# Moving one ScalarE operation, the sum of s_i and mask, behind four softmax divisions in a graph-attention kernel

## The chip, the cores and the metric

The kernel runs on one core of a Trainium2 chip. A core has a matrix engine (TensorE, PE in the profile; its weight loads are listed apart as PEld), three engines for elementwise work (VectorE or DVE, ScalarE or ACT, GpSimd or POOL), and a queue, SyncE or SP, from which nearly all transfers here are issued. Each engine goes through its own list of instructions, and semaphores tie the lists together. The metric is the device time of one execution in microseconds. Before the change it is 2422.0 us, the median of three runs (2419.04, 2422.00, 2422.31).

## What is computed

There are 128 graphs of 128 nodes with 512 features, and two layers. Layer 0 is multi-head attention with 8 heads, masked by the adjacency matrix. Layer 1 is a single-head graph attention. Each is followed by a residual addition and a layer normalization without weights. Cut to what matters:

```
# layer 0
q, k, v = x @ Wq + bq, x @ Wk + bk, x @ Wv + bv          # 8 heads of 64
logits  = where(adj > 0, q k^T / 8, -1e9)
attn    = softmax(logits, axis=-1)
x       = layernorm(x + relu((attn v) @ Wo + bo))

# layer 1
Wh  = x @ W
e   = leaky(s_i[:, None] + s_j[None, :])     # s_i = Wh @ a1, s_j = Wh @ a2, leaky slope 0.2
e   = where(adj > 0, e, -9e15)
att = softmax(e, axis=1)                     # over the senders i
x   = layernorm(x + leaky(att @ Wh))
```

## The kernel before, in words

Everything is done in float32. The work on a graph ("block" b) is cut into stages, and one loop over `t` runs different stages of different graphs side by side: the softmax of layer 0 for block t, its attention for block t - 1, layer 0's output product for a pair of blocks starting at t - 3 (odd t), the product with W for the pair at t - 6 (even t), and the edge softmax of layer 1 for blocks near t - 6. The projections q, k, v are made for four blocks at a time, and their pieces are spread over four steps. The loop runs to t = 123; the last four blocks follow a written list of pieces (`PLAN`). The order of instructions on every engine is the order of the program text (`manual_schedule`); no scheduler moves anything.

All large products use Strassen's scheme: seven products p1 to p7 of half-size blocks instead of eight, accumulated in PSUM banks with the roles y, w and x. The same bank y serves p1, p6, p7 and p4 in turn, so ScalarE has to copy it out (`t0`, `t2`, `t3`) before TensorE may write it again:

- `group_product` (matmuls at line 364, copies at 341 and 345, `st_` tiles) makes q, k, v. The weights of v don't fit on chip; their seven blocks come through a ring of three tiles `wv_n` (line 405).
- `pair_product` (matmuls at line 445, copies `pr_t` at line 456) makes the output product of layer 0 in odd steps and x @ W in even ones. Its pieces are taken one by one with `pair()`. The copy `t3` is made in the `pair()` between divisions 5 and 6; the product p4 overwrites the bank it reads.

In x @ W (class `LayerOne`), W has one column more, so that s_i and s_j come out as the last columns of the two halves of `wh`. For the even block of a pair the half with s_i is added by VectorE (line 766) in the same step in which it is used; for the odd block ScalarE copies it (line 764) late in the even step, for use in the following odd one.

The softmax of layer 0 (class `Softmax`, tile `pa`, 128 queries x 8 heads x 128 keys): VectorE adds the mask to the scores (line 530) and takes the maxima (539); ScalarE takes the exponential of each head and its sum (`exp`, line 550, eight instructions); VectorE takes the reciprocals of the sums for heads 0 to 3 and 4 to 7 (`reciprocals`, line 560); ScalarE multiplies each head by its reciprocal (`divide`, line 564, eight instructions). `pa` is then stored to memory (571), read back in blocks (577), and transposed by VectorE (581).

The edge softmax (class `Edge`): `sender` (line 792) is a ScalarE activation that adds s_i, a column of `wh`, to the mask and makes the tile `e`. `store_sender` (800) stores it, `fetch_sender` (806) reads it back in blocks as `ez`, and `turn_blocks` (811) transposes it on VectorE at the start of the next step. Then `add` (814) adds s_j, and the maxima (819, 821), exponential (825), and division (829, 830) follow.

Within a step the SP queue issues the output store (859), the store of `e` (800), often a weight block (405), the store of `pa` (571), the four reads of `ez` (806) and the four reads of `pa` (577), in this order.

Of the kernel before, what the change touches and what calls it, by code (L numbers as in the profile page):

```python
# [24 lines left out]
def kernel(  # L25
# [114 lines left out]
    def load_blocks(*args, **kwargs):  # L140
        for load in block_loads(*args, **kwargs):
            load()
# [4 lines left out]
    def right_blocks(t):  # L147

        return [
            lambda: nc.vector.tensor_sub(t[2], t[2], t[0]),  # L150
            lambda: nc.vector.tensor_sub(t[5], t[3], t[2]),
            lambda: nc.vector.tensor_sub(t[4], t[5], t[0]),
            lambda: nc.vector.tensor_sub(t[6], t[1], t[5]),
        ]

    def places(w):
        return [w[:, n] for n in range(7)]

    def columns(w):
        return w[:, 0:2], w[:, 2:4]  # L160
# [23 lines left out]
    def load_bias():  # L184
        nc.sync.dma_start(bo_b, bo.partition_broadcast(P))
        return [lambda: nc.vector.tensor_sub(bo_b[:, HALF:], bo_b[:, HALF:], bo_b[:, :HALF])]
# [61 lines left out]
    def load_x(b):  # L248
        X[b] = spread(x[b])

    def load_residual(b):

        X1[b] = work.tile([P, D], F32, name="x1", bufs=7)
        nc.sync.dma_start(X1[b], x[b])

    def transpose_x(b):
        g, j = divmod(b, GROUP)
        if j == 0:
            XT[g] = big.tile([P, NC, GROUP * P], F32, name="xT")
        transpose_blocks(XT[g][:, :, j * P : (j + 1) * P], X.pop(b))  # L260

    def sum_x(g):
        sums = big.tile([P, 3, 2, 2 * P], F32, name="xS")
        XS[g], ops = left_blocks(XT[g], sums)
        return lambda: [op() for op in ops]
# [219 lines left out]
    def load_mask(b):  # L485
        MF[b] = small.tile([P, P], I32, name="adj", bufs=2)
        nc.sync.dma_start(MF[b], adj[b])

    def mask_float(b):
        a = MF[b]  # L490
        MF[b] = small.tile([P, P], BF16, name="mf", bufs=9)
        nc.scalar.copy(MF[b], a)

    def mask(b):
        nc.vector.tensor_scalar(MF[b], MF[b], 0.0, BIG, ALU.is_le, ALU.mult)
# [366 lines left out]
    def on(b):  # L862
        return 0 <= b < B
# [19 lines left out]
    def turn_x1(t):  # L883
        layer = zero.pop((t - 4) // 2)
        layer.transpose(0)
        layer.transpose(1)
        sums.append(layer)

    def x1_sums():
        while sums:  # L890
            sums.pop().sum(0, 1, 2, 3)
# [3 lines left out]
    sm = fin = edge = coming = none  # L895

    def x_turns(t):
        if t < 0:
            return {-3: (), -2: (4,), -1: (5, 6, 7)}[t]
        return [b for b in [(), (t + 7, t + 8), (t + 8,), (t + 8,)][t % GROUP] if on(b)]  # L900
# [64 lines left out]
    for t in range(-3, END):  # L965
        pair_steps = []
        if t % GROUP == 1 and on(t + 3):
            rest = group_steps
            group_steps, v_pieces, fetch_v = products((t + 3) // GROUP)
            group_steps = rest + group_steps  # L970
        if t % 2 == 1 and on(t - 3):
            pair_steps = zero[(t - 3) // 2] = LayerZero((t - 3) // 2)
            pair_steps = pair_steps.steps()
        if t % 2 == 0 and on(t - 6):
            pair_steps = LayerOne((t - 6) // 2).steps()

        def group(n=1):
            for _ in range(min(n, len(group_steps))):
                group_steps.pop(0)()
            for _ in range(min((3 if t == -3 else 2 if t >= 1 else 1) * n, len(chores))):  # L980
                chores.pop(0)()

        def w1_chores(n):
            for op in [w1_sums.pop(0) for _ in range(n)]:
                op()

        def pair(n=1):
            for _ in range(min(n, len(pair_steps))):
                pair_steps.pop(0)()

        if on(t + 1):
            load_mask(t + 1)
        if t == 0:
            load_blocks(Wo, columns(wo), nc.sync, spread_rows=False)
            late_chores = right_blocks(places(wo)) + load_bias()
        if t == 1:
            w1_loads, w1_sums = load_w1()
            for chore in late_chores:
                chores += [w1_loads.pop(0), chore]
            chores += w1_loads  # L1000

        last, sm = sm, Softmax(t, first_homes if t in (0, 2, 4) else None) if on(t) else none
        sm.scores()
        coming.turn_blocks()
        if t % 2 == 1 and on(t - 3):
            zero[(t - 3) // 2].by()
            zero[(t - 3) // 2].bw()
        if later and t > 4:
            later.pop().go_back()
        if t == 5:  # L1010
            group(2)
        if t < 3:
            sm.maxima()
            group(2)
            if on(t - 2):
                load_residual(t - 2)
            if t == 0 and on(GROUP):
                sum_x(1)()
            sm.exp(0, 1, 2, 3)
            last.transpose()  # L1020
            group()
            sm.reciprocals(0)
            sm.exp(4, 5, 6, 7)
            if t == 1:
                group()
            sm.reciprocals(1)
            sm.divide(0, 1, 2, 3)
            group()
            sm.divide(4, 5, 6, 7)
            if t == 1:  # L1030
                group()
            if on(t + 1):
                mask_float(t + 1)
        elif t == 4:

            layer = later.pop()
            sm.maxima()
            group()
            layer.apply(0)
            load_residual(2)  # L1040
            if on(8):
                sum_x(2)()
            sm.exp(0, 1)
            group()
            sm.exp(2, 3, 4, 5)
            last.transpose()
            group()
            layer.store(1)
            layer.store(0)
            layer.fetch(1)  # L1050
            layer.fetch(0)
            sm.exp(6, 7)
            group()
            sm.reciprocals(0)
            sm.reciprocals(1)
            sm.divide(0, 1, 2, 3, 4, 5, 6, 7)
            mask_float(5)
        else:
            sm.maxima()
            group()  # L1060
            if t == 5:
                turn_x1(4)
                x1_sums()
            edge = coming
            edge.add()
            fin.residual()
            if on(t - 2):
                load_residual(t - 2)
            edge.maxima()
            fin.stats()  # L1070
            fin.rstd()
            x1_sums()
            if t % GROUP == 0 and on(t + GROUP):
                sum_x(t // GROUP + 1)()
            pair()
            sm.exp(0, 1, 2, 3)
            edge.exp()
            pair()
            sm.exp(4, 5)
            last.transpose()  # L1080
            group()
            sm.reciprocals(0)
            pair()
            sm.exp(6)
            fin.apply()
            fin.store()
            sm.exp(7)
            edge.divide()
            pair()
            sm.reciprocals(1)  # L1090
            coming = Edge(t - 6) if on(t - 6) and t + 1 < END else none
            coming.sender()
            coming.store_sender()
            sm.divide(0, 1, 2, 3)
            if t == 3:
                w1_chores(4)
            group()
            sm.divide(4, 5)
            pair()
            sm.divide(6, 7)  # L1100
            if on(t + 1):
                mask_float(t + 1)
            group()
            if t in (3, 5):
                w1_chores(4 if t == 3 else 8)
        sm.store()
        if t >= 6:
            coming.fetch_sender()
        sm.fetch()
        for b in x_turns(t):  # L1110
            transpose_x(b)
        for b in x_turns(t + 1):
            load_x(b)
        if on(t + 1):
            mask(t + 1)
        pair(2)
        if t % 2 == 0 and on(t - 6):
            turn_x1(t)
        if t not in (0, 4):
            group(21 if t % GROUP == 0 else 1)  # L1120
        fin = edge
        fin.product()
        fin.copy()

        last.attend()
        last.copy()
        if t % 2 == 0:
            last.sum(0, 1, 2, 3)
# [183 lines left out]
```

## Time and profile before

| engine | busy us | share of the span |
|---|---|---|
| TensorE, matmuls | 2368.3 | 98% |
| TensorE, weight loads | 1975.1 | 82% |
| VectorE | 1827.5 | 76% |
| ScalarE | 1515.2 | 63% |
| GpSimd | 812.7 | 34% |

The profiled span is 2418.1 us at a mean granted TensorE clock of 0.998. Some groups of instructions that the text uses:

| operation, line | times | one, us |
|---|---|---|
| sender `e` on ScalarE, 792 | 117 | 0.398 (median) |
| division `pa` on ScalarE, 564 | 1008 | 0.392 (mean) |
| exponential `pa` on ScalarE, 550 | 1008 | 0.394 (mean), and 0.191 for reading the sum |
| copy `pr_t` on ScalarE, 456 | 375 | 0.366 (mean) |
| store of `e`, 64 KB, 800 | 117 | 1.8 to landing (median) |
| reading `ez`, 4 x 16 KB, 806 | 468 | 2.2 to landing (median) |
| weight block `wv_n`, 256 KB, 405 | 224 | 2.8 to landing (median) |

A "wait" in the profile is idle time of an engine just before an instruction, put down to what released it last. A line of the timeline gives the start in us, the duration in us, the engine, the line of the kernel, the operation, the tiles (out<-in), the shapes, how often it was repeated, and in brackets the idle time before it. Instructions of one engine overlap a little: each starts while the one before it is still draining. The ends of matmuls are modelled, so the distance between two starts tells more of TensorE than a duration does.

### The profile page before, as it was taken

How to read it: one execution, taken by the hardware profiler on the slowest of the kernel's cores; microseconds unless marked ns; L12 is line 12 of the kernel's file. 1: busy time of each engine (PE TensorE's matmuls, PEld its weight loads, DVE VectorE, ACT ScalarE, POOL GpSimd, SP SyncE). 2: the span in 40 equal slices, each digit the busy share in tenths (PEclk: the TensorE clock that was granted, in tenths of full speed). 3: DMA queues.
4: the chain of work that ended last, by engine and by line, in shares of the span. 5: the costliest groups of instructions: out<-in, count | busy, mean ns of one | idle time of the engine just before them, and what ended most of it. 6: DMA issues, size and time to landing. Idle time of an engine off the chain costs nothing.

```text
span 2418.1 us, 44124 instructions
## 1 busy us (share of the span) xinstructions
PE 2368.3 (98%) x13350; PEld 1975.1 (82%) x13350; DVE 1827.5 (76%) x3719; ACT 1515.2 (63%) x5463; POOL 812.7 (34%) x1195
## 2 busy tenths in 40 slices
PE   8999999999999999999999999999999999999996
PEld 7788888888888888888888888888888888888874
DVE  5677787787777777877877777778778777777777
ACT  3656666566666666665666666666666666666685
POOL 1223333233343333332333433333323334333335
PEclk9999999999999999999999999999999999999999
DMA  6555555555545545545545555455555455554552
GB/s 195 177 159 155 173 159 160 179 158 156 178 153 174 168 147 181 162 158 176 159 155 177 154 173 169 148 179 155 168 175 158 155 177 157 169 172 146 161 168 98
DMA packets 435502, 395.32 MB, mean 163 GB/s; under 512 B 108216, under 2 KB 339264, under 8 KB 435264
## 3 DMA queue, kind: packets, MB, share of 16 engines
q1 hardware_dynamic: 434688, 391.97, 52.2%
q8 instruction: 107, 1.75, 0.3%
q14 instruction: 131, 1.07, 0.1%
q10 hardware_dynamic: 576, 0.52, 0.1%
HBM read 248.58 MB, written 143.72 MB: 162 GB/s over the span
## 4 chain that ended last, share of the span: by engine, by line
PE 78%; ACT 9%; DVE 5%; DMA 3%; issue 2%; POOL 1%; SPq 1%; POOLq 0%; DVEq 0%; ACTq 0%
PE st_y L364 22%; PE p_y L445 15%; PE st_w L364 12%; PE p_w L445 7%; PE lg L516 5%; PE p_oT L594 5%; PE st_x L364 4%; PE p_h L835 4%; PE p_x L445 3%; ACT pa L550 3%; ACT pa L564 3%; DMA pa_dram<-pa 1%; DVE z L659 1%; DVE att L830 1%; DMA x_dram<-x 1%
## 5 line engine op out<-in xcount | busy, mean ns | idle before, releaser
L550 ACT ACTIVATE pa<-pa,nmax 128x128 f32<-128x128 f32 x1008 | 392.6, 394 | 12.3 <-DVE nmax L539 12.2
L644 POOL TENSOR_SCALAR ve<-mv 128x1 f32<-128x1 f32 x256 | 70.2, 274 | 857.3 <-DVE mv L640 848.5
L564 ACT ACTIVATE pa<-pa,rs 128x128 f32<-128x128 f32 x1008 | 327.1, 392 | 6.8 <-DVE rs L560 6.8
L273 POOL TENSOR_TENSOR oS<-oT 128x256 f32<-128x256 f32 x63 | 45.8, 728 | 658.0 <-ACT oT L608 658.0
L530 DVE TENSOR_TENSOR pa<-lg,mf 128x512 f32<-128x512 f32 x252 | 162.0, 684 | 99.0 <-PE lg L516 98.3
L456 ACT COPY pr_t<-p_y 128x257 f32<-128x257 f32 (+1 forms) x375 | 137.3, 366 | 134.7 <-PE p_y L445 130.5
L341 ACT COPY st_t<-st_y 128x512 f32<-128x512 f32 x192 | 110.5, 575 | 138.6 <-PE st_y L364 138.6
L550 ACT ACTIVATION_READ_ACCUMULATOR pa<-pa,nmax 128x1 f32 x1008 | 192.5, 191 | 0.0
L646 POOL TENSOR_TENSOR rstd<-ve,mhalf 128x1 f32<-128x1 f32 x256 | 177.0, 691 | 21.4
L594 PEld LDWEIGHTS p_oT<-paT,v 128*64 128x64 f32 x2016 | 107.5, 136 | 91.6 <-PE st_y L364 44.0
L608 ACT ACTIVATE oT<-p_oT,b_cols 128x128 f32<-128x128 f32 x504 | 144.1, 368 | 60.5 <-PE p_oT L594 59.2
L345 ACT ACTIVATE st_t<-st_y,b_cols 128x256 f32<-128x256 f32 x192 | 80.6, 471 | 160.7 <-PE st_y L364 160.7
L581 DVE STREAM_TRANSPOSE paT<-paz 128x1024 f32<-128x1024 f32 x126 | 156.9, 1245 | 13.2 <-DMA paz<-pa_dram 12.0
L539 DVE TENSOR_REDUCE nmax<-pa 128x8 f32<-128x1024 f32 x126 | 153.7, 1220 | 4.4
L766 DVE TENSOR_TENSOR wh<-p_w,pr_t 128x257 f32<-128x257 f32 x122 | 51.8, 425 | 129.8 <-ACT pr_t L456 84.3
L516 PE MATMUL lg<-kT,qT 64*128 64x128 f32 x2048 | 148.7, 285 | 0.0
L516 PEld LDWEIGHTS lg<-kT,qT 64*128 64x128 f32 x2048 | 124.2, 187 | 22.9 <-issue 22.9
L445 PE MATMUL p_y<-w,x1T 128*128 128x257 f32 x496 | 130.8, 386 | 7.5 <-ACT pr_t L456 7.4
L594 PE MATMUL p_oT<-paT,v 128*64 128x128 f32 x2016 | 137.9, 279 | 0.0
L445 PE MATMUL p_y<-wo,oT 128*128 128x256 f32 x504 | 129.6, 380 | 0.9 <-ACT pr_t L456 0.8
L445 PE MATMUL p_y<-w,x1S 128*128 128x257 f32 x496 | 128.0, 380 | 1.9 <-ACT pr_t L456 1.9
L445 PE MATMUL p_y<-wo,oS 128*128 128x256 f32 x504 | 129.4, 379 | 0.0
(201 smaller groups left out, 6025.8 us busy)
## 6 DMA issues: line engine op xcount, KB each, us to landing
pa_dram<-pa SPq DMA_DIRECT2D x126, 512.0 KB, 2.6
paz<-pa_dram SPq DMA_DIRECT2D x504, 128.0 KB, 2.8
wv_n<-wv SPq DMA_DIRECT2D x224, 256.0 KB, 2.8
x<-in_x_dram SPq DMA_DIRECT2D x128, 256.0 KB, 3.1
x_dram<-x SPq DMA_DIRECT2D x128, 256.0 KB, 2.5
xz<-x_dram SPq DMA_DIRECT2D x512, 64.0 KB, 2.0
xz<-in_x_dram SPq DMA_DIRECT2D x496, 64.0 KB, 2.2
out_dram<-z SPq DMA_DIRECT2D x120, 256.0 KB, 2.3
```

Source lines behind the costliest of these rows:

```text
L364: nc.tensor.matmul(p[:, m, :], lhs, rhs, start=start and m == 0 and kc == 0, stop=True, skip_group_check=True,)
L445: nc.tensor.matmul(p[:, :width], xs()[n][:, kc, :], w[:, PLACE[n], kc, :], start=start and kc == 0, stop=True, skip_group_check=True,)
L456: nc.scalar.copy(t[:, :width], p[:, :width])
L516: nc.tensor.matmul(self.lg[r][:, c, :], q[rows, c, cols], k[rows, c, cols], start=c == 0, stop=True, skip_group_check=True,)
L530: nc.vector.tensor_add(by_head[:, r * NC : (r + 1) * NC], self.lg[r].rearrange("p c (b k) -> p c b k", b=4), mf.unsqueeze(1).to_broadcast( ...
L539: nc.vector.tensor_reduce(self.nmax, by_head, AX.XY, ALU.max, negate=True)
L550: nc.scalar.activation(self.pa[:, :, h, :], self.pa[:, :, h, :], AF.Exp, bias=self.nmax[:, h : h + 1], accum_out=self.sums[:, h : h + 1],)
L564: nc.scalar.activation(self.pa[:, :, h, :], self.pa[:, :, h, :], AF.Copy, scale=self.rs[:, h : h + 1])
L581: nc.vector.transpose(self.paT.rearrange("p h (a i) -> p a h i", i=32), self.paz.rearrange("p a (h k) -> p a h k", k=32),)
L594: nc.tensor.matmul(self.oT[r * HD : (r + 1) * HD, c, :], v[:, h * HD : (h + 1) * HD], self.paT[:, r * NC + c, :], start=c == 0, stop=True, ...
L608: nc.scalar.activation(OT[pair][:, c, h * P : (h + 1) * P], self.oT[:, c, :], AF.Identity, bias=b_cols[:, 1, c : c + 1],)
L646: nc.gpsimd.tensor_tensor(self.r, ve, mhalf, ALU.pow)
```

## The change

On ScalarE the sender of the edge softmax stood ahead of the divisions of heads 0 to 3 of the softmax of layer 0. Now these four divisions come first. The sender needs `wh`, which VectorE adds in the same step when t is even; the divisions need the reciprocals of the first four sums, which are taken earlier. The order of ScalarE's work follows from the order of the lines, so moving one line is the whole change; the sender's store stays behind the sender, and the lists of the other engines and of the SP queue keep their order.

```
             edge.divide()
             pair()
             sm.reciprocals(1)
+            sm.divide(0, 1, 2, 3)
             coming = Edge(t - 6) if on(t - 6) and t + 1 < END else none
             coming.sender()
             coming.store_sender()
-            sm.divide(0, 1, 2, 3)
             if t == 3:
                 w1_chores(4)
             group()
```

More of the change, by code (lines that the diff above doesn't have):

```diff
@@ L1090 @@
             sm.reciprocals(1)
+            sm.divide(0, 1, 2, 3)
             coming = Edge(t - 6) if on(t - 6) and t + 1 < END else none
@@ L1093 @@
             coming.store_sender()
-            sm.divide(0, 1, 2, 3)
             if t == 3:
```

## The prediction

> **What bounds the kernel now.** I read the busy table first, then who waited for whom, then the chain of work that ended last, then the timeline of one stretch.
>
> ```profile
> PE 2368.3 (98%) x13350; PEld 1975.1 (82%) x13350; DVE 1827.5 (76%) x3719; ACT 1515.2 (63%) x5463; POOL 812.7 (34%) x1195
> ```
>
> TensorE (PE) is busy nearly all the time, so only what lets PE start earlier can shorten the span; ScalarE (ACT) has slack on average. Taking an idle stretch off ACT is worth something only where PE stands still behind it. The list of waits says where that is (columns: who waited, on whom; total us, times, longest):
>
> ```profile
> ACT e L792 <- DVE wh L766: 61.1, 57, 1.9
> ...
> PEld p_y L445 <- ACT pr_t L456: 18.6, 26, 1.2
> ...
> PE p_y L445 <- ACT pr_t L456: 10.0, 27, 1.9
> ...
> PEld st_y L364 <- DMA wv_n<-wv: 6.3, 9, 1.4
> ```
>
> Line 792 is the sender, the operation that the change moves: ACT stood idle 61.1 us ahead of it, in 57 of 117 executions, until VectorE (DVE) had finished `wh`, whose last column is s_i. Going through them in the timeline: 29 waits are 1.85 to 1.87 us (every step with t a multiple of 4, t = 8 to 120) and 28 are 0.23 to 0.26 us (with one of 0.07) in the other even steps. Odd steps don't wait: there ACT itself wrote `wh` in the step before. The second and third rows are PE (PEld: its weight loads) waiting for ACT's copy `pr_t`. The chain of work over 1054 to 1070 us (start, duration, what; the step t = 56) ties the two together:
>
> ```profile
> 1062.92 1.10 DVE att L830
> 1064.02 0.35 DVE wh L766
> ...
> 1064.38 0.40 ACT e L792
> 1064.79 1.75 ACT pa L564 x6
> 1066.54 0.27 ACT pr_t L456
> ...
> 1066.85 1.14 PE p_y L445 x4
> ```
>
> The chain leaves PE, goes through DVE's `wh`, the sender, six divisions (line 564) and the copy `pr_t`, and returns to PE. So here the sender's wait does reach PE. The timeline of the same step (start, duration, engine; in brackets the idle time before, and what ended it):
>
> ```profile
> 1058.58 1.89 PE L364 MATMUL st_y<-wv_n,xS 128*128 128x256 f32 x8
> ...
> 1060.31 1.03 PE L445 MATMUL p_y<-w,x1S 128*128 128x257 f32 x4
> ...
> 1061.18 1.03 PE L445 MATMUL p_x<-w,x1T 128*128 128x257 f32 x4
> ...
> 1062.33 0.19 ACT L550 ACTIVATION_READ_ACCUMULATOR pa<-pa,nmax 128x1 f32 x1
> ...
> 1063.77 1.03 PE L445 MATMUL p_y<-w,x1S 128*128 128x257 f32 x4
> ...
> 1064.38 0.40 ACT L792 ACTIVATE e<-mf,wh 128x128 f32<-128x128 bf16 x1 [1.86 <-DVE wh L766]
> ...
> 1064.64 1.89 PE L364 MATMUL st_y<-wv_n,xS 128*128 128x256 f32 x8
> 1064.69 1.85 ACT L564 ACTIVATE pa<-pa,rs 128x128 f32<-128x128 f32 x6
> ...
> 1066.45 0.35 ACT L456 COPY pr_t<-p_y 128x257 f32<-128x257 f32 x1
> ...
> 1066.85 1.14 PE L445 MATMUL p_y<-w,x1T 128*128 128x257 f32 x4 [0.32 <-ACT pr_t L456]
> ...
> 1067.83 1.03 PE L445 MATMUL p_w<-w,x1T 128*128 128x257 f32 x4
> ```
>
> ACT is free at 1062.52. The reciprocals of heads 0 to 3 have been ready since 1061.61 (line 560, 1061.48 + 0.13), so four divisions could run, but they stand behind the sender until 1064.38.
>
> **What the Trainium skill says.** "Perfetto Trace Analysis", section "Tensor Engine Instruction (MATMUL, LD_WEIGHTS)": ScalarE and VectorE run strictly first in, first out, while the end of a matmul is estimated. The trace agrees on the first (ready divisions lie 1.86 us behind a waiting sender); because of the second I measure PE's loss from start to start. "ScalarE: Activation LUTs", section "Rules for kernel authors", budgets about 0.3 us per operation plus 0.83 ns per element, an estimate of 0.41 us for 128 columns; the trace has a median of 0.389 us for a division, of which the pipeline hides some: six take 1.85 us, 0.31 us from start to start, and that is what I use. "SBUF — State Buffer", section "The DMA setup-cost knee": a transfer has a nearly fixed cost of about 2 us; here e_dram<-e, 64 KB, lands in 1.5 to 4.9 us, median 1.8.
>
> **The change part by part.** No instruction is added or removed; on ACT the sender changes places with divisions 0 to 3. The order on PE, DVE, POOL and the SP queue stays.
>
> *Steps with t a multiple of 4.* The divisions start at 1062.55 and are through by 1062.55 + 4 x 0.31 + 0.1 = 1063.9. The sender still waits for DVE until 1064.38, but only 0.5 us. Behind it now stand two divisions, not six, ahead of `pr_t`: 4 x 0.31 = 1.24 us less, so the copy runs at 1065.21 rather than 1066.45. What it reads, p7 in `p_y`, is complete at 1063.77 + 1.03 = 1064.80, and divisions 4 and 5 need the second reciprocal, which DVE has ready at 1064.43 (1064.27 + 0.16). So `pr_t` is done at about 1065.6. PE wants it only when `st_y` is over.
>
> What PE loses today: from the start of `st_y` to the next `p_y` is 1060.31 - 1058.58 = 1.73 us without a wait and 1066.85 - 1064.64 = 2.21 with it, 0.48 lost; from that `p_y` to its successor 1061.18 - 1060.31 = 0.87 against 1067.83 - 1066.85 = 0.98, another 0.11, a weight load that no longer lies beside a matmul. Together 0.59 us, and with the copy 0.5 us ahead of need (weights are wanted at about 1066.1) all of it goes.
>
> How often: among the 29 steps, 24 show PE idle behind `pr_t`, 20 by 0.31 to 0.32 us and four by 0.16 to 0.24. In the other five PE was held just before by a weight block (wv_n) that had not landed, and `pr_t` was then in time: no gain. 20 x 0.59 = 11.8. The four: 0.50 each (0.59 less what the idle time is shorter), 2.0. Sum 13.8 us.
>
> *Other even steps.* ACT saves its 0.26 us; PE doesn't wait for ACT there, so nothing. *Odd steps.* The sender doesn't wait; the same five operations in another order end at the same time. Nothing. The same for t = 6, whose `pr_t` wait has no sender wait ahead of it. The last four blocks run from a written plan that calls the sender separately: unchanged.
>
> *What comes later.* The sender's store (e_dram) is behind it, and on the SP queue behind that a weight block, the store of the weights `pa` and the reading back, ez. Both bounds of the delay: zero with t a multiple of 4 (the sender starts at 1064.38 as before), and up to 4 x 0.31 = 1.24 us elsewhere. At t = 55 SP was held by the output store anyway (sender at 1044.96, e_dram issued 1046.29), so it moves only about 0.4 us; at t = 53 and 54 about 1 us. ez is issued only after `pa` is stored (1012.66 and 1030.56 in those steps), 1.6 to 2.6 us after the new issue. Its consumer is DVE's block transpose at the start of the next step; at t = 55 that started at 1036.04, after waiting 1.84 us for ez, and the addition behind it waits until 1037.26 for PE's scores: 1037.26 - 1036.04 - 0.30 = 0.92 us of slack. I take zero for all this; the other end is 0.3 us of lateness in the 29 steps like t = 55, some 9 us, if ez lands over 1 us later.
>
> **Rivals.**
> 1. *The weight block takes the wait's place.* wv_n lands close to its use: in nine steps PE's weight load did wait for it, five times enough to hold PE (0.46 to 0.96 us). For it: the stall that goes away sits right after this wait, so nothing will absorb a late block any more. Against: the chain to wv_n starts from PE in the same and the preceding step, ahead of the stall, so its slack doesn't shrink. If half of the 24 gains go: 2422.0 - 6.9 = 2415.
> 2. *PE is held by something else at the same place*, for instance the free bank for p_w, which DVE reads after `pr_t`: no gain, 2422. Against: that reading moves earlier with `pr_t`.
> 3. *Slower.* ez comes late, DVE starts the scores' addition late, exponentials and divisions follow, and PE waits in odd steps. With 0.6 us in 29 + 29 odd steps, 35 us, less 13.8: 2443; with the 9 us above still 2417. For it: ez is already waited for (1.84 us). Against: 0.92 us of slack, and transfers ahead of e_dram set much of its landing.
> 4. *More than forecast.* `pa` is stored 1.1 us earlier every fourth step, the queue clears, and the five weight waits (0.8 to 1.2 us each with the exposed load) go too: 13.8 + 5 gives 2403.
>
> **How the numbers follow.** Forecast 2422.0 - 13.8 = 2408: chance 0.68. Rival 1: 0.14, of which two thirds stay faster by over 0.2% (below 2417.2). Rival 2: 0.05. Rival 3: 0.06, of which one sixth would end within 0.2%. Rival 4: 0.07. Faster 0.68 + 0.09 + 0.07 = 0.84; same 0.05 + 0.05 + 0.01 = 0.11; slower 0.05. The range goes from rival 4 to half of rival 1's side and the run-to-run spread before (2419.0 to 2422.3): 2403 to 2418.
>
> **What would show it.** In the waits: the sender's 61.1 us falls to some 15 (29 x 0.5), and PE's wait for `pr_t` from 10.0 us to about 2.8 (its share before 172 us). In the timeline: four divisions ahead of the sender, `pr_t` about 1.2 us earlier against `st_y`, 1.73 us from `st_y` to `p_y`. Wrong would be: more than nine waits for wv_n, a new PE wait at p_y or p_w, or longer waits of DVE for ez (46.8 us in 35 now).

## The result, and the profile after

The changed kernel takes 2407.58 us (median of four runs, 2406.89 to 2408.14) against 2421.62 (2419.04 to 2422.31): a ratio of 0.9944, 95% interval 0.9927 to 0.9961. The profiled span fell from 2418.1 to 2405.3 us.

The page has the same 44124 instructions and nearly the same busy times. What changed is the chain that ended last: TensorE holds 89% of it where it held 78% before, and ScalarE 2% where it held 9%.

```profile
PE 2363.0 (98%) x13350; PEld 1980.5 (82%) x13350; DVE 1829.4 (76%) x3719; ACT 1516.7 (63%) x5463; POOL 797.4 (33%) x1195
...
PE 89%; DMA 2%; DVE 2%; ACT 2%; issue 2%; POOL 2%; SPq 1%; DVEq 0%; POOLq 0%; ACTq 0%
```

The waits of the changed kernel (total us, times, longest), to set beside those shown before:

```profile
ACT e L792 <- DVE wh L766: 20.6, 29, 0.9
...
PEld st_y L364 <- DMA wv_n<-wv: 7.1, 8, 2.2
...
PE st_y L364 <- DMA wv_n<-wv: 4.3, 5, 1.8
...
PE p_y L445 <- ACT pr_t L456: 2.8, 3, 1.9
...
PEld p_y L445 <- ACT pr_t L456: 1.7, 2, 1.2
```

In the kernel before, TensorE's matmuls waited for weight blocks as follows:

```profile
PE st_y L364 <- DMA wv_n<-wv: 3.3, 5, 1.0
```

ScalarE's wait ahead of the sender fell from 61.1 to 20.6 us and from 57 to 29 times. TensorE's wait for `pr_t` is left in three places, all ahead of 150 us, and the two waits of weight loads that are left lie there too. The waits for weight blocks are still there.

The timeline of the changed kernel in the step t = 56, the one shown before:

```profile
1056.12 0.19 ACT L550 ACTIVATION_READ_ACCUMULATOR pa<-pa,nmax 128x1 f32 x1
1056.22 1.27 ACT L564 ACTIVATE pa<-pa,rs 128x128 f32<-128x128 f32 x4
...
1058.17 0.40 ACT L792 ACTIVATE e<-mf,wh 128x128 f32<-128x128 bf16 x1 [0.69 <-DVE wh L766]
...
1058.43 1.89 PE L364 MATMUL st_y<-wv_n,xS 128*128 128x256 f32 x8
1058.48 0.68 ACT L564 ACTIVATE pa<-pa,rs 128x128 f32<-128x128 f32 x2
...
1059.06 0.35 ACT L456 COPY pr_t<-p_y 128x257 f32<-128x257 f32 x1
...
1060.16 1.03 PE L445 MATMUL p_y<-w,x1T 128*128 128x257 f32 x4
...
1061.03 1.03 PE L445 MATMUL p_w<-w,x1T 128*128 128x257 f32 x4
```

Read it from start to start. The four divisions begin as soon as the last exponential is done, and the sender behind them waits 0.69 us. The copy `pr_t` starts 1059.06 - 1058.43 = 0.63 us after `st_y`, where it was 1066.45 - 1064.64 = 1.81: 1.18 us sooner. From `st_y` to `p_y` is now 1.73 us (2.21 before) and from `p_y` to `p_w` 0.87 (0.98 before). So 0.59 us per such step are gone, to the last digit what the prediction took from its comparison. The groups of four steps below give the same: 73.78 - 73.19 = 0.59.

Whole times carry a scatter from the first steps, which is described in the last section, so all kernels are also compared by the stretch from the first matmul of the scores of t = 8 to that of t = 120 in the profiled run. It has 28 steps with t a multiple of 4, so it can be cut into 28 groups of four steps, each from scores to scores. The last column gives the median length of a group in which TensorE waited neither for a weight block nor, in an odd step, for a copy `pr_t`. Stretch and groups come from one trace of each kernel. The ratios of the experiments are to executions of the kernel before that were made beside them, in three batches (medians 2422.5, 2423.0 and 2422.2 us).

| kernel | time, us | ratio to before (95%) | start of t = 8 | t = 8 to 120, us | against before | four undisturbed steps, us |
|---|---|---|---|---|---|---|
| before | 2421.6 | | 168.4 | 2066.9 | | 73.78 |
| changed | 2407.6 | 0.9944 (0.9927 to 0.9961) | 168.6 | 2053.4 | -13.5 | 73.19 |
| fourth_only | 2408.0 | 0.9940 (0.9927 to 0.9954) | 167.8 | 2053.8 | -13.1 | 73.19 |
| others_only | 2424.3 | 1.0008 (1.0000 to 1.0016) | 169.8 | 2068.6 | +1.7 | 73.78 |
| one_ahead | 2415.6 | 0.9973 (0.9962 to 0.9984) | 170.5 | 2059.9 | -7.0 | 73.48 |
| two_ahead | 2411.4 | 0.9953 (0.9940 to 0.9965) | 172.6 | 2055.9 | -11.0 | 73.20 |
| sum_first | 2407.8 | 0.9941 (0.9927 to 0.9954) | 167.8 | 2053.1 | -13.8 | 73.19 |
| sender_last | 2423.7 | 0.9999 (0.9991 to 1.0008) | 172.0 | 2066.1 | -0.8 | 73.19 |
| weights_first | 2403.9 | 0.9924 (0.9912 to 0.9937) | 173.5 | 2049.4 | -17.5 | 73.19 |
| weights_first_before | 2421.3 | 0.9992 (0.9984 to 1.0001) | 171.1 | 2065.8 | -1.1 | 73.78 |
| last_and_weights | 2404.8 | 0.9930 (0.9918 to 0.9943) | 169.8 | 2052.2 | -14.7 | 73.19 |
| last_in_thirds | 2421.9 | 0.9998 (0.9990 to 1.0006) | 170.7 | 2062.1 | -4.8 | 73.19 |
| last_in_others | 2415.5 | 0.9969 (0.9958 to 0.9980) | 171.4 | 2058.1 | -8.8 | 73.19 |

### The profile page after: what moved, and what is told of

It is laid out like the page before. It is cut to its first block, busy times and chain, and to the rows that moved or that the text cites. A ratio compares the mean times of both kernels' runs of the same rounds, so it can differ in the third digit from the quotient of the medians.

```text
span 2405.3 us, 44124 instructions
## 1 busy us (share of the span) xinstructions
PE 2363.0 (98%) x13350; PEld 1980.5 (82%) x13350; DVE 1829.4 (76%) x3719; ACT 1516.7 (63%) x5463; POOL 797.4 (33%) x1195
## 4 chain that ended last, share of the span: by engine, by line
PE 89%; DMA 2%; DVE 2%; ACT 2%; issue 2%; POOL 2%; SPq 1%; DVEq 0%; POOLq 0%; ACTq 0%
PE st_y L364 26%; PE p_y L445 17%; PE st_w L364 13%; PE p_w L445 8%; PE st_x L364 6%; PE lg L516 5%; PE p_oT L594 5%; PE p_x L445 4%; PE p_h L835 4%; ACT pa L564 1%; DMA wv_n<-wv 1%; ACT pa L550 1%; DMA x_dram<-x 1%; DMA pa_dram<-pa 1%; DMA paz<-pa_dram 0%
## 5 line engine op out<-in xcount | busy, mean ns | idle before, releaser
L564 ACT ACTIVATE pa<-pa,rs 128x128 f32<-128x128 f32 x1008 | 333.9, 394 | 7.4 <-DVE rs L560 7.4
L364 PE MATMUL st_y<-wv_n,xS 128*128 128x256 f32 x512 | 123.4, 385 | 6.8 <-DMA wv_n<-wv 4.3
```

Of the source, the lines that this page charges most:

```text
L364: nc.tensor.matmul(p[:, m, :], lhs, rhs, start=start and m == 0 and kc == 0, stop=True, skip_group_check=True,)
L564: nc.scalar.activation(self.pa[:, :, h, :], self.pa[:, :, h, :], AF.Copy, scale=self.rs[:, h : h + 1])
```

## The experiments

My theory was that the gain is TensorE's stall behind `pr_t` in the steps with t a multiple of 4, and nothing else. The rivals were that it comes from ScalarE's smaller waits elsewhere, or from the store of `e`, which now comes later.

**Where: the change in some steps only.** fourth_only makes the change where t is a multiple of 4, others_only everywhere else.

```
+            if t % 4 == 0:                      # others_only: != 0
+                sm.divide(0, 1, 2, 3)
             coming = Edge(t - 6) if on(t - 6) and t + 1 < END else none
             coming.sender()
             coming.store_sender()
-            sm.divide(0, 1, 2, 3)
+            if t % 4 != 0:                      # others_only: == 0
+                sm.divide(0, 1, 2, 3)
```

> The divisions stand ahead of the sender only in steps with t a multiple of 4; in all others the sender stays first. My theory (the gain is the idle time of TensorE behind pr_t in those steps alone): the same as the changed kernel, 2407.6 us, within 1.5 us. Rival A (the gain comes from ScalarE's 0.26 us in the other even steps, or from the later store of e in all steps): half of the gain or less, 2414 us or more.

> The complement: the divisions first in all steps but those with t a multiple of 4. My theory: no gain, 2421.6 us within 1.5 us, with TensorE waiting for pr_t in 24 or so steps as before. Rival A: 2414 us or less. Rival B (the later store of e does harm that the gain covers in the full change): slower than before by 1 us or more.

fourth_only has the whole gain, 2408.0 us and 13.1 us in the stretch; others_only has none of it. TensorE's waits in others_only:

```profile
PE p_y L445 <- ACT pr_t L456: 10.1, 25, 1.9
...
PE st_y L364 <- DMA wv_n<-wv: 5.0, 8, 1.2
```

The wait for `pr_t` is back at its old size. So rival A falls. others_only is slower than before by a hair (1.0008, the interval touching 1), with eight waits for weight blocks, 5.0 us, where the kernel before had five, 3.3 us in all. Rival B, that the later store does some harm in the other steps, is not ruled out by it; yet the full change, which has these later stores too, is as fast as fourth_only, 2053.4 against 2053.8 us in the stretch. In others_only 1.15 of the 1.7 us lost in the stretch lie in the four steps from t = 28 alone, where TensorE waited 0.75 us for a copy `pr_t` of layer 0 in the odd step 31. Whether this and the three more waits come from the later store or from scatter stays open: fourth_only has a smaller wait of the same kind (0.28 us, step 19), though the stores of its odd and other even steps are not moved.

**How much: fewer divisions ahead of the sender.**

```
+            sm.divide(0)                        # two_ahead: 0, 1
             coming = Edge(t - 6) if on(t - 6) and t + 1 < END else none
             coming.sender()
             coming.store_sender()
-            sm.divide(0, 1, 2, 3)
+            sm.divide(1, 2, 3)                  # two_ahead: 2, 3
```

> Only division 0 goes ahead of the sender, in all steps. My theory: pr_t comes 0.31 us earlier, while TensorE needs 0.48 us to be free of the wait; so 0.31 us per step in 24 steps, 7.4 us: 2414.2 us, and TensorE's wait for pr_t shrinks from 0.32 us to under 0.05 us by the profile while its weight loads still wait some 0.4 us. Rival C (what counts is only that the sender is not the first to wait, whatever stands behind it): the full gain, 2407.6 us. Rival D (the gain is four divisions' worth, each a quarter): 2418 us.

> Divisions 0 and 1 go ahead of the sender. My theory: 0.62 us earlier is more than the 0.59 us that TensorE loses per step, so the whole gain: 2407.6 us within 1.5 us, no wait of TensorE for pr_t after the first 172 us. Rival D: 2414.6 us.

The waits for `pr_t` in one_ahead:

```profile
PEld p_y L445 <- ACT pr_t L456: 11.0, 26, 0.7
...
PE p_y L445 <- ACT pr_t L456: 2.3, 3, 1.9
```

TensorE's matmuls no longer show the wait after the first steps, but its weight loads still do, 0.42 us each (0.72 before): here a stall of 0.3 us is seen in the weight load alone. From start to start `st_y` to `p_y` is 1065.39 - 1063.48 = 1.91 us at t = 56, between the 2.21 and the 1.73 of the two kernels. The stretch is 7.0 us shorter; 7.4 was expected. With two divisions ahead, no wait for `pr_t` is left in the loop, and 11.0 us are gained. The whole time is 3.8 us over what I expected. The profiled run is 5.9 us longer than that of the changed kernel: 4.0 us of it lie ahead of t = 8, and the stretch is 2.5 us longer; TensorE waited for weight blocks in eight steps rather than five. Where none was late, four steps take 73.20 us, against 73.19 with four divisions ahead, so two divisions do bring the whole gain of a step. The gain is neither all at once nor a quarter for each of the four divisions (rivals C and D fall): four undisturbed steps fall from 73.78 us to 73.48 with the first division and to 73.20 with the second, 0.3 us each, and the next two add nothing.

**By other means: the wait made shorter, the order kept.** In sum_first the sender stays ahead of the divisions, and VectorE takes its sum `wh` before the edge softmax's reciprocal and division.

```
-            edge.divide()
             pair()
+            edge.divide()
             sm.reciprocals(1)
```

> ScalarE's order is that of the kernel before (the sender first). Instead VectorE's sum wh is taken ahead of the reciprocal and the division of the edge softmax (rt, att), so that the sender is released about 1.1 us earlier. My theory (the cause is the time at which ScalarE gets past the sender, by whatever means): pr_t about 1.1 us earlier in steps with t a multiple of 4, more than the 0.59 us needed, so the same gain as the change: 2407.6 us within 2 us, and no wait of TensorE for pr_t after 172 us. Rival E (the gain comes from the later sender, for instance from the later store of e, or from divisions that run earlier): no gain, 2421.6 us.

The waits of sum_first:

```profile
ACT e L792 <- DVE wh L766: 19.0, 29, 0.7
...
PE p_y L445 <- ACT pr_t L456: 2.4, 3, 1.9
```

2407.8 us, 13.8 us in the stretch: the same gain, with ScalarE's instructions in the old order, and in the steps with t a multiple of 4 the store of `e` comes 1.2 us earlier than in the kernel before (median, from the first scores of the step), not later. So it's neither the order of ScalarE's work as such nor the later store that brings it, but the moment at which ScalarE is past the sender. Rival E falls.

**What is left: the weight blocks.** Of the stalls of TensorE in the loop, the changed kernel has only the late wv_n blocks. In weights_first the SP queue issues the block ahead of the eight reads of x_dram, which otherwise wait there for their store to land; weights_first_before does the same to the kernel before.

```
         def go_back(self):
             self.apply(0)
             self.store(0)
-            self.fetch(1)
-            self.fetch(0)
...
+        back = none
         if later and t > 4:
-            later.pop().go_back()
+            back = later.pop()
+            back.go_back()
...
         else:
             sm.maxima()
             group()
+            back.fetch(1)
+            back.fetch(0)
```

> The changed kernel, and in addition the two reads of x_dram (xz) are issued behind the weight block wv_n of the same step rather than ahead of it, so that the block starts up to 4 us earlier. My theory (all that holds TensorE in the loop now are the late weight blocks): the five waits, 4.3 us and about 0.28 us each for the exposed weight load, go: 2402 us within 2 us. Rival H (the reads that now come later hold VectorE or TensorE instead): 2407.6 us or more.

> The same early weight block in the kernel before, with the sender still ahead of the divisions. My theory (in five steps the late block hid TensorE's wait for pr_t, and a step pays for one of the two): the block's wait goes (3.3 us and 5 x 0.28 us, 4.7 us in all), the wait for pr_t appears in its place (5 x 0.59 us, 2.9 us), so 29 waits for pr_t from t = 8 on and a time 1.8 us shorter than before, 2419.8 us. Rival I (the two waits add up): 4.7 us shorter, 2416.9 us, and 24 waits for pr_t.

In weights_first, the queue in the step t = 56 reads:

```profile
1053.20 1.22 SPq L710 DMA_DIRECT2D x_dram<-x  x1
1054.96 0.32 SPq L405 DMA_DIRECT2D wv_n<-wv  x1
1055.58 3.64 SPq L238 DMA_DIRECT2D xz<-x_dram  x8
```

The block is issued at 1054.96 for a product that starts at 1062.57, 7.6 us ahead; in the changed kernel it was 1058.43 - 1055.08 = 3.4 us. TensorE waits for nothing between t = 8 and t = 120: 2049.4 us for 28 steps, or 73.19 us for four, the distance from group to group in the undisturbed changed kernel (its senders of t = 12 and t = 16 start at 252.25 and 325.44). The time is 2403.9 us, the best of all, 4.0 us shorter in the stretch than the changed kernel; 2402 was expected, within 2 us. (The profiled run, 2407.2 us, is the slowest of the five, and it reached t = 8 4.9 us later than the changed kernel's.) By whole times alone the two aren't told apart for certain: the intervals of their ratios to before overlap.

In weights_first_before the waits for `pr_t` are these:

```profile
PE p_y L445 <- ACT pr_t L456: 11.2, 30, 1.9
```

From t = 8 on it is in every one of the 29 steps, 0.32 us each, where the kernel before had it in 24: with the late block gone, the stall that it hid came out. A step paid for one of the two, not for both, as the prediction had it. That is why the same edit gains 4.0 us on the changed kernel and 1.1 us (1.8 expected) on the one before, in the stretch; the whole time of weights_first_before can't be told from that of the kernel before. The two kernels with the early block also show the change by itself, with no late weight block in either: 2065.8 - 2049.4 = 16.4 us over 28 steps, 0.59 us each.

**How far the sender can go.** In sender_last, sender and store stand behind all eight divisions.

```
-            coming.sender()
-            coming.store_sender()
...
             sm.divide(6, 7)
+            coming.sender()
+            coming.store_sender()
```

> The sender and its store go behind all eight divisions, ahead of the store of pa. My theory: pr_t has no sender ahead of it, so TensorE's waits for it stay away; the store of e comes some 1.2 to 2 us later than in the changed kernel, ez by about as much, and the slack of 0.92 us at VectorE's block transpose is used up in part of the odd steps: VectorE waits for ez more than 45 us in total, and the time lies between 2408 and 2414 us. Rival F (the store of e has no bearing at all): 2407.6 us. Rival G (ez is on the edge already): 2421 us or more.

My expectation missed: 2423.7 us, no faster than before, though no steady wait for `pr_t` is left. The waits of sender_last:

```profile
DVE e_turned L811 <- DMA ez<-e_dram: 82.2, 45, 4.8
...
PE st_y L364 <- DMA wv_n<-wv: 12.7, 14, 1.6
```

TensorE waited 12.7 us for weight blocks, in 14 steps, and VectorE 82.2 us for `ez`, in 45 (45.3 in 36 with the change). Counted from the first scores of the step, the store of `e` is issued 1.5 to 2.5 us later than in the changed kernel and the reading of `ez` 1.0 to 1.5 us later (medians of the steps with the same t modulo 4). Three more kernels ask by which road the late store costs time: the same with the early weight block, and the sender last in only those steps where t = 3 modulo 4, or in all but those.

> Sender and store behind all eight divisions, and the weight block issued ahead of the reads of x_dram. With the sender last alone, TensorE waited 12.7 us for weight blocks. Theory K (the late store of e costs time through the SP queue: ez, pa, x_dram and the weight block behind it): with the early weight block that route is closed, so 2404 to 2408 us and no wait for wv_n in the loop. Theory L (the cost runs through VectorE's wait for ez, the late addition and the divisions): the early block changes little, 2415 us or more.

> As the changed kernel, but with sender and store behind all eight divisions in steps with t = 3 modulo 4. Theory K, in the form that the chain to the weight block begins with that step's store of e: most of the 16 us of harm, 2416 to 2424 us, and TensorE waits for wv_n 9 us or more. Theory L: harm in proportion to the steps, a quarter, 2411.6 us.

> The complement: sender and store last in all steps but those with t = 3 modulo 4. Theory K: 2407 to 2411 us, wv_n waited for some 4 to 6 us as in the changed kernel. Theory L: three quarters of the harm, 2419.6 us.

last_and_weights is fast, 2404.8 us: no wait for wv_n, and most of the cost is gone. Behind all eight divisions the sender costs 12.7 us in the stretch with the late block (sender_last against the changed kernel) and 2.8 with the early one (last_and_weights against weights_first), although VectorE still waits nearly as long for `ez`:

```profile
DVE e_turned L809 <- DMA ez<-e_dram: 77.5, 53, 4.4
```

last_in_thirds has the cost, 8.7 us in the stretch against the changed kernel, with 9.6 us of waiting for wv_n in 14 steps. Its chain of work shows the road (start, duration, what):

```profile
533.35 2.74 DMA e_dram<-e
...
537.42 1.85 DMA ez<-e_dram
...
541.27 4.09 DMA x_dram<-x
...
547.20 3.25 DMA wv_n<-wv
...
550.49 1.56 PE st_y L364 x6
```

`e` is stored just ahead of `pa`, so the queue stands about 2 us (534.14 to 536.11) until it has landed before it can issue `ez`; `ez` is late for VectorE's transpose, which stands ahead of the normalization that x_dram stores; the queue waits again for that store, and the weight block stands behind it. Seventeen microseconds after the late store, TensorE waits.

So theory K holds for the greater part. But last_in_others is not free: 2415.5 us, 4.7 us over the changed kernel in the stretch, when K said 2407 to 2411. In the stretch the two parts, 8.7 and 4.7, add up to about the 12.7 of sender_last; by the medians of the whole times, 14.3 and 7.9 against 16.1, they don't (the profiled run of last_in_thirds was the second fastest of its thirteen), so the sizes are rough. In last_in_others the cost takes the road of theory L:

```profile
376.57 0.31 DVE L811 STREAM_TRANSPOSE e_turned<-ez 128x128 f32<-128x128 f32 x1 [5.34 <-DMA ez<-e_dram]
...
379.34 0.40 ACT L550 ACTIVATE pa<-pa,nmax 128x128 f32<-128x128 f32 x1 [1.77 <-DVE nmax L539]
...
387.50 1.13 PE L445 MATMUL p_y<-wo,oT 128*128 128x256 f32 x4 [0.74 <-ACT pr_t L456]
```

In this odd step VectorE waited 5.34 us for `ez`, ScalarE's exponentials began late, and TensorE waited for `pr_t`, here of layer 0. TensorE's matmuls have such waits in four odd steps (five pieces, 3.1 us), and its weight loads alone in a fifth. The five groups of four steps with them are 5.0 us longer in all than undisturbed ones; the groups with late weight blocks are 3.7 us longer, 4.0 in the changed kernel. So the 4.7 us are these odd steps. In last_and_weights nearly all of the 2.8 us that are left lie in such groups, and in last_in_thirds all the loss lies in groups with late weight blocks. So the late store costs time by both roads here: mostly by the weight block when it is late in the steps with t = 3 modulo 4, by VectorE and the copy when it is late in the others.

## Why the prediction was right

- *What bounds the kernel.* Right. Where nothing else disturbs them, four steps take 73.78 us in the three kernels that keep the stall behind `pr_t` (before, others_only, weights_first_before), 73.48 with half of it (one_ahead), and 73.19 or 73.20 in all that are free of it. What still sets kernels apart in the stretch lies in groups with a late weight block or a late copy in an odd step.
- *The loss per step, 0.59 us.* Right, 0.48 + 0.11 measured in the same step. It had to be read from start to start: the wait printed beside the matmul was 0.32 us, so adding up the printed waits would have given half.
- *0.31 us for a division.* A little too long: 1.85 us divided by six counts the end of the last one in full. From the first division to the copy behind the six it was (1066.45 - 1064.69) / 6 = 0.29. So four divisions are 1.17 us rather than 1.24, and 1.18 were measured. Nothing hung on it: TensorE needed the copy only some 0.6 us sooner.
- *How often, and the sum of 13.8 us.* Right in size, 14.0 us between the medians and 13.5 in the stretch, but the make-up differs, and that the parts cancel is luck. The 24 groups of four steps in the stretch that lost time to `pr_t` gained 12.2 us, not 13.8: in two of them, at t = 72 and t = 104, the weight block was now late, and smaller losses came at 92 and 108. The four groups counted as no gain gained 1.3 us, because the block of t = 60 came in time and that of t = 84 nearly so.
- *The sender still waits 0.5 us.* Slightly off: 0.69, so 20.6 us in all where some 15 were forecast. The four divisions are through sooner than taken: they last 1.27 us together, not 1.34, and begin 0.09 us before the last exponential's sum is read out. ScalarE's wait isn't on TensorE's path, and it cost nothing.
- *Other even and odd steps: nothing.* Right (others_only).
- *What comes later, taken as zero.* Right for this change. The store of `e` moved by 0.4 to 0.8 us in the steps where t is not a multiple of 4, but the reading of `ez` behind the store of `pa` was issued at the same time within 0.04 us (medians), which was one of the two reasons given. The other, 0.92 us of slack at VectorE's transpose, was not the whole of what such a delay can touch: sender_last shows that with `ez` 1.0 to 1.5 us later the whole gain is lost, mostly by the SP queue and the weight block, which the prediction had not connected with the store of `e`.
- *Rival 1, the weight block takes the wait's place.* In part, and not on balance. It did so at t = 72 and t = 104; but there were five waits before (3.3 us in matmuls) and five after (4.3 us), three of them in the same steps. This agrees with the argument that the block's slack is counted from TensorE's work ahead of the stall, but no experiment tested that argument.
- *Rivals 2 and 3, another wait at the same place, or a late `ez`.* Neither came: between t = 8 and t = 120 TensorE waits for no other engine at `p_w`, and VectorE waited 45.3 us for `ez` in 36 steps, where it had been 46.8 in 35.
- *Rival 4, `pa` stored 1.1 us earlier clears the queue.* Half right and without a visible gain: the store moved from 2.60 to 1.44 us after that of `e` (medians over the steps with t a multiple of 4), but then `ez` began 1.12 instead of 0.41 us after `pa`, because `e` had not landed yet. Of the 1.16 us that the queue gained, 0.7 went into the next wait, and the five waits for weight blocks stayed.

## What to carry to other kernels

When an engine's wait stands ahead of work that is ready, ask first which wait of the bounding engine lies behind it. Here 61 us of idle ScalarE were worth 14 us, because in only 24 of its 57 waits TensorE ran dry, and only for 0.59 of the 1.86 us. Size such a gain by the distance between two starts on the bounding engine, once with the stall and once without. And when two waits can hold the same point, the removal of one is worth only what it lasts beyond the other: the early weight block gained 1 us before the change and 4 us after it.

## What was not expected of the hardware

The stretch ahead of t = 8 took between 167.8 and 173.5 us in the profiled runs, although these kernels differ little there. Already at the start of t = 4, ahead of which all of them give every engine the same work in the same order, they lie 3.8 us apart (97.0 to 100.8 us). That is as much as several of the effects asked for here, and so whole times of this kernel were not read without the stretch behind. The cause was not looked into.

The landing of `e` does not follow its issue alone. In the step t = 56 of the kernel before it took 4.0 us, against a median of 1.8, when four transfers of 256 KB had been issued in the 3.3 us ahead of it. They alone don't explain it: in the changed kernel the same four were issued in the 3.5 us ahead, and `e` landed in 2.0 us. The cause stays open.
